# Half-transposes in turns with quarter rows, shared products ahead of the last row, an earlier flag load

## The chip, the cores and the metric

The kernel runs on one core of a Trainium2 chip. The metric is device time in microseconds (us) of one execution. The kernel before took 286.78 us, the median of three runs (286.23 to 288.38).

A core has five engines with a queue each. TensorE (PE in the profile; PEld is its weight load) multiplies matrices into PSUM, VectorE (DVE) and ScalarE (ACT) work element by element and copy out of PSUM, GpSimd (POOL) here mostly issues indirect DMAs, SyncE (SP) issues plain DMAs. An engine takes its instructions in the order of the program and waits on semaphores for the others.

## The reference

One graph convolution with relations and one mixture of experts, on 625 rows of 1024 numbers in float32. Cut to what matters:

```python
# 625 nodes, 20000 edges sorted by dst, 2 edge types
h   = layernorm(x)
n   = ln_weight * h / sqrt(mean(h*h) + 1e-6)
out = n @ W_root + bias                                  # 1024 -> 286
for r in range(2):
    msg  = n[src] @ W_rel[r] * (edge_type == r)
    out += segment_sum(msg, dst) / max(count, 1)
x   = x + h + elu(out) @ wo_weight                       # 286 -> 1024

h2  = layernorm(x)
shared = mean_s( gelu(h2 @ sW1[s] + sb1[s]) @ sW2[s] + sb2[s] )     # 2 shared, 1024 -> 256 -> 1024
gates  = h2 @ rW + rb                                    # 8 experts
w      = softmax of the two largest gates of a row, 0 elsewhere
moe    = sum_e w[:, e] * ( gelu(h2 @ W1[e] + b1[e]) @ W2[e] + b2[e] )
return x + shared + moe
```

## The kernel before

The 625 rows are five row tiles of 125. `sparse_kernel` computes everything under the assumption that edges and expert loads stay within certain sizes; it leaves a flag, and after it `gnn_ffn_kernel` reads the flag into registers and branches to `dense_kernel` where it is above zero (which it isn't with these inputs). The stages of `sparse_kernel`, with the span's time at which the trace shows them:

1. **0 to 94 us, graph convolution.** Edge counts, projection, aggregation.
2. **94 to 122 us, output rows.** The loop over `s` (L1114) does `output_proj(s)` for a row tile; DVE and ACT make the row tile's layer norm h2, two steps later `to_columns` (L835) transposes it on TensorE, eight transposes p_t of 125x125, into `h2T`. h2 is also written to HBM as `h2d`.
3. **122 to 158 us, routing beside the shared experts.** `gate`, `route` and `slots` are a long DVE chain with a few small matmuls: gate logits, the two best experts (`sel`), ranks within an expert (p_rank), the token index of each slot (p_tok), `tok` for whole rows and `tok4` for quarters of rows. TensorE fills its time with `shared_in` (L1202): for each shared expert i, half t and column cut (0..313, 313..625) eight products p_sh (k = 0..7) and a Gelu. The scheduler places these products among the small matmuls; four of the first eight stand ahead of the last row tile's transposes. A register load on TensorE and ACT reads the tiles' expert numbers (`ej`).
4. **158 to 207 us, first expert layer.** Tokens are sorted to 11 tiles of 128 slots: seven whole tiles of one expert (numbers 4 to 10), three of two halves of 64 (0, 1, 2), one of four quarters of 32 (3). They are taken in the order 4, 5, 6, 0, 7, 1, 8, 2, 9, 10, 3. The loop over `s` gives three steps, each a tile behind the one before: `fetch`, `expert_in`, `expert_mid`. `fetch` gathers the tile's rows from `h2d` by POOL's indirect DMA and turns them to columns `xsT`, in one of two ways. A tile in `by_quarters` takes four gathers of 128 x 256 (L1424) and one stream transpose on DVE (L1429). The others take one gather of 128 x 1024 (L1434), eight transposes p_x on TensorE (L1441) into two PSUM banks, a copy of the first four on ACT (L1447) and of the last four on DVE (L1445). Quarter tiles are the places 1, 3, 5, 7, 9, 10 of the order, so the first tile is a whole one. `copy_w1` (L1451) copies second and further experts' w1 for the divided tiles on ACT. `expert_in` (L1458) is the matmuls p_h (16 records for a whole tile) and a DVE copy `hj` (L1466). `expert_mid` (L1471) transposes `hj` on TensorE (p_hT) and applies Gelu on ACT. `xs` has three buffers, `xsT` two; PSUM banks are five for p_x, p_sh and p_yj (`ps_acc`) and three for p_h and p_hT (`ps_mm`).
5. **207 to 245 us, second expert layer.** p_yj (L1522), for each tile two halves of 512 columns; copies `ys` on DVE and ACT (L1526, L1528); a scatter to `yt` in HBM by POOL (L1530).
6. **245 to 288 us, combination.** The shared experts' second layer p_o (L1577, with the biases' row L1579), two halves for each row tile and three parts for the last. SP loads the scattered rows back (g, L1541). `add` (L1549) is a chain on DVE, each held behind the one before: x plus p_o, then x plus weight times g. `store` (L1559) writes a row tile, 112 rows by SP and 13 by ACT. All p_o are held behind the last p_yj (`made`). The flag is loaded to the engines' registers at the end (L1594), then the branch (L1595) and the closing waits (L1624).

What sets the order: `tc.issue_after` holds an instruction behind another one by hand; the rest of each engine's order comes from a scheduler that sees the program as written, and buffers of pools, which add waits on those who used the memory before. `xt`, the pool of `xsT`, is opened after `sh_in` (the shared experts' weights and h2T) is closed.

Of the kernel before, what the change touches and what calls it, by code (L numbers as in the profile page):

```python
# [8 lines left out]
F32 = mybir.dt.float32  # L9
# [9 lines left out]
N = 625  # L19
# [7 lines left out]
TP = 125  # L27
NT = N // TP
KD = D // 128
EP = 125  # L30
EC = E // EP
# [12 lines left out]
NJ = 11  # L44
# [409 lines left out]
def sparse_kernel(  # L454
# [24 lines left out]
    nc = tc.nc  # L479
# [15 lines left out]
    def ps_acc(name):  # L495
        return psum[0].tile([128, 512], F32, tag="acc", name=name, bufs=nacc[0])
# [10 lines left out]
    rows = pool(gnn, "rows", NT)  # L507
# [60 lines left out]
    ident = const.tile([128, 128], F32, name="ident")  # L568
# [311 lines left out]
    made = {}  # L880
# [147 lines left out]
    turned = []  # L1028
# [82 lines left out]

    load_w1(range(2))
    sh_in = ExitStack()
    for s in range(NT + 2):  # L1114
        if s == 0:
            aggregate(NT - 1, 1)
            elu(NT - 1)
            elu_columns(NT - 3)
            cnts.close()
            rt = pool(sh_in, "rt", side="right")  # L1120
            shi = pool(sh_in, "shi", side="right")
            sw1 = shi.tile([128, NS, KD, H], F32, name="sw1")
            for i in range(NS):
                nc.sync.dma_start(sw1[:, i], sW1[i].rearrange("(k p) h -> p k h", p=128))
            load_w1(range(2, NE))
            h2T = shi.tile([128, KD, N], F32, name="h2T")
        if s < NT:
            output_proj(s)
        if s == 0:
            check()  # L1130
        if s < 2:
            elu_columns(NT - 2 + s)
        if 0 <= s - 2 < NT:
            to_columns(s - 2, h2s[s - 2], h2T, False)
    gnn.close()
# [6 lines left out]
    CUTS = ((0, 313), (313, N))  # L1142


    gT = rt.tile([128, 2, TP], F32, name="gT")
    gates = const.tile([TP, NT, NE], F32, name="gates")
# [54 lines left out]

    def shared_in(i, t, then=lambda: None):  # L1202
        b = KD + i * HK + t
        for a, z in CUTS:
            if a:
                then()
            p = ps_acc(f"p_sh_{i}_{t}_{a}")
            for k in range(KD):
                nc.tensor.matmul(p[:, : z - a], sw1[:, i, k, t * 128 : (t + 1) * 128],  # L1209
                                 h2T[:, k, a:z], start=(k == 0), stop=(k == KD - 1))  # L1210
            nc.scalar.activation(shT[:, i, t, a:z], p[:, : z - a], AF.Gelu, bias=vT[:, b : b + 1])


# [164 lines left out]
    def quarter_rows():  # L1378
        own4 = rt.tile([128, 4, 4, QC], F16, tag="above", name="own4")
        tf = rt.tile([128, NJ], F16, name="tf")  # L1380
        for a in range(4):
            nc.scalar.copy(own4[:, a], ident[:, None, a * QC : (a + 1) * QC].to_broadcast([128, 4, QC]))
        with tc.issue_after(named.ins):
            nc.vector.tensor_copy(tf, tok)
        q4 = ps_mm("p_tok4")
        for a in range(4):
            nc.tensor.matmul(q4[:, a * NJ : (a + 1) * NJ], own4[:, a].rearrange("p b r -> p (b r)"), tf,
                             start=True, stop=True)
        nc.vector.tensor_scalar(tok4.rearrange("p a j -> p (a j)"), q4[:, : 4 * NJ], 4.0, quad,
                                op0=ALU.mult, op1=ALU.add)  # L1390

    gate()
    route()
    named = slots()
    weights_T()
    shared_in(1, 0, quarter_rows)
    shared_in(1, 1)
    sh_in.close()

# [15 lines left out]
        return ((0, 128, e_of[NH2 + j - 1]),)  # L1415

    xsT, p_hs, w1m = {}, {}, {}
    acts, turned = [], []

    def fetch(j):  # L1420
        if j in by_quarters:
            xs = io.tile([128, 4, D // 4], F32, tag="io", name=f"xs_{j}")
            for a in range(4):
                nc.gpsimd.indirect_dma_start(  # L1424
                    out=xs[:, a], out_offset=None, in_=h2d.rearrange("n (b f) -> (n b) f", b=4),
                    in_offset=bass.IndirectOffsetOnAxis(ap=tok4[:, a, j : j + 1], axis=0))
            t_ = xt.tile([128, KD, 128], F32, tag="xsT", name=f"xsT_{j}")
            with tc.issue_after(turned[-1].ins):
                nc.vector.transpose(t_.rearrange("p k (a r) -> p a k r", a=4), xs.rearrange("p a (c k) -> p a k c", k=KD))  # L1429
            xsT[j] = t_  # L1430
            copy_w1(j)
            return
        xs = io.tile([128, D], F32, tag="io", name=f"xs_{j}")
        nc.gpsimd.indirect_dma_start(  # L1434
            out=xs, out_offset=None, in_=h2d,
            in_offset=bass.IndirectOffsetOnAxis(ap=tok[:, j : j + 1], axis=0))
        t_ = xt.tile([128, KD, 128], F32, tag="xsT", name=f"xsT_{j}")
        for g in range(2):
            p = ps_acc(f"p_x{g}_{j}")
            for k in range(4):  # L1440
                nc.tensor.transpose(p[:, k * 128 : (k + 1) * 128], xs[:, 4 * g + k :: KD], ident)  # L1441
            o = t_[:, 4 * g : 4 * g + 4, :]
            pv = p.rearrange("p (k n) -> p k n", k=4)
            if g:
                turned.append(nc.vector.tensor_copy(o, pv))  # L1445
            else:
                acts.append(nc.scalar.copy(o, pv))  # L1447
        xsT[j] = t_
        copy_w1(j)

    def copy_w1(j):  # L1451
        for jj, a, e in copies.get(j, ()):
# [28 lines left out]

    whole = range(NM2, NJ)
    tiles = (*whole[:3], 0, whole[3], 1, whole[4], 2, *whole[5:], NH2)
    by_quarters = [tiles[i] for i in (1, 3, 5, 7, 9, 10)]
    copies = {}
    for i, (j, a, e) in zip((1, 3, 5, 6, 8, 9), ((j, a, e) for j in tiles for a, _, e in parts(j)[1:])):
        copies[tiles[i]] = [(j, a, e)]
    for s in range(NJ + 2):
        if s < NJ:
            fetch(tiles[s])  # L1490
        if 0 <= s - 1 < NJ:
            expert_in(tiles[s - 1])
        if 0 <= s - 2 < NJ:
            expert_mid(tiles[s - 2])
# [52 lines left out]
    added = []  # L1547

    def add(*args):  # L1549
        with ExitStack() as order:  # L1550
            if added:
                order.enter_context(tc.issue_after(added[-1].ins))
            added.append(nc.vector.scalar_tensor_tensor(*args, op0=ALU.mult, op1=ALU.add))  # L1553

    def add_experts(d):
# [2 lines left out]

    def store(d, at):  # L1559
        for g, eng in zip(PARTS, (nc.sync, nc.scalar)):  # L1560
            eng.dma_start(out[d * TP + g.start : d * TP + g.stop, at], x1[g, d, at])

    banks = 0
    for d in range(NT):
        if d == LATE:
            for i in range(d, NT):
                add_experts(i)
        own = slice(d * TP, (d + 1) * TP)
        for at in ((0, 512), (512, D)) if d < NT - 1 else ((0, 512), (512, 768), (768, D)):
            n = at[1] - at[0]  # L1570
            at = slice(*at)
            p = (ps_mm if banks % 8 > 4 else ps_acc)(f"p_o_{d}_{at.start}")
            banks += 1
            with tc.issue_after(made.ins):
                for i in range(NS):
                    for k in range(HK):
                        nc.tensor.matmul(p[:TP, :n], shT[:, i, k, own], sw2[:, i, k, at],  # L1577
                                         start=(i == 0 and k == 0), stop=False)
                nc.tensor.matmul(p[:TP, :n], wT[:, own], b23[:, at], start=False, stop=True)  # L1579
            add(x1[:, d, at], p[:TP, :n], 1.0 / NS, x1[:, d, at])  # L1580
            if d == NT - 1:
                store(d, at)
        if d < LATE:
            add_experts(d)
        if d < NT - 1:
            store(d, slice(0, D))


def gnn_ffn_kernel(tc, *args):
    nc = tc.nc  # L1590
    with tc.tile_pool(name="flags", bufs=1) as flags:
        flag = flags.tile([1, 1], I32, name="flag")
        sparse_kernel(tc, flag, *args)
        off = nc.values_load(flag, min_val=0, max_val=EC * 4 + 1)  # L1594
        with tc.If(off > 0):  # L1595
            dense_kernel(tc, *args)

# [30 lines left out]
```

## Time and profile before

| what | value |
|---|---|
| median of three runs | 286.78 us |
| the profiled execution's own time | 290.18 us |
| its span | 288.4 us |
| granted TensorE clock, mean | 0.993 |
| TensorE busy | 277.2 us (96%) |
| DVE busy | 171.8 us (60%) |
| ACT busy | 100.2 us (35%) |
| POOL busy | 65.1 us (23%) |

Busy time is the union of an engine's instructions. The span runs from the first to the last instruction of the profiled execution; the time outside it, 1.8 us here, belongs to the start and end of the launch. A row of a timeline gives start, duration, engine, line, operation, output from input, the number of instructions put together, and in brackets how long the engine was idle before it and who released it. Successive matmuls overlap in the records, so a row's duration is longer than its share of the engine's time.

### The profile page before, as it was taken

To read this page: it belongs to the slowest core of one execution; us is meant where nothing else is said; L and a number is where in the kernel's file an instruction comes from. 1 tells how busy PE (TensorE), PEld (TensorE's weight loads), DVE (VectorE), ACT (ScalarE), POOL (GpSimd) and SP (SyncE) were. 2 spreads that over 40 slices of the span, in tenths; PEclk is the share of its full clock that TensorE was granted. 3 is DMA by queue.
4 is the path that set the end of the run, shared out by engine and by line. 5 is a ranking of instruction groups with operands and counts; after the bars stand their busy time and mean duration, and the time that the engine had idled before them with its cause. 6 is when DMAs were issued, how large, how long until landed. Compare 5 with 4: busy or idle time off the path is not lost.

```text
span 288.4 us, 4459 instructions
## 1 busy us (share of the span) xinstructions
PE 277.2 (96%) x1531; PEld 186.5 (65%) x1531; DVE 171.8 (60%) x433; ACT 100.2 (35%) x232; POOL 65.1 (23%) x128
## 2 busy tenths in 40 slices
PE   8999999999999999899999988999999999999991
PEld 6877777788888455677777877788543344444460
DVE  6899999999874898657800522446143111159820
ACT  3366328243642422453011414854397111000000
POOL 9910110000000124320151656541022222100000
PEclk9999999999999999999999999999999999999997
DMA  7999960000002999996999344321185545399441
GB/s 230 358 333 368 403 216 28 0 0 2 1 0 74 383 391 426 423 403 206 418 406 400 101 145 130 128 60 53 45 338 231 213 190 220 133 374 376 150 142 43
DMA packets 22107, 61.58 MB, mean 214 GB/s; under 512 B 2490, under 2 KB 8317, under 8 KB 21056
## 3 DMA queue, kind: packets, MB, share of 16 engines
q1 hardware_dynamic: 16106, 44.31, 41.3%
q0 software_dynamic: 5680, 16.58, 16.0%
q10 hardware_dynamic: 294, 0.35, 0.6%
q8 instruction: 14, 0.23, 0.3%
q14 instruction: 13, 0.11, 0.1%
HBM read 43.19 MB, written 18.82 MB: 215 GB/s over the span
## 4 chain that ended last, share of the span: by engine, by line
PE 82%; DVE 12%; issue 3%; ACT 1%; DVEq 0%; ACTq 0%
PE p_pr L944 18%; PE p_yj L1522 13%; PE p_o L1577 12%; PE p_h L1462 11%; PE p_sh L1209 11%; PE p_agg L961 5%; PE scrap L1024 2%; PE p_y L1007 2%; DVE xh L1011 2%; PE cnt L923 2%; DVE xsT L1429 1%; DVE st L776 1%; DVE h L749 1%; PE p_t L841 1%; PE p_gate L1155 1%
## 5 line engine op out<-in xcount | busy, mean ns | idle before, releaser
L944 PE MATMUL p_pr<-wg,nT 128*125 128x286 f32 x240 | 61.7, 408 | 0.5 <-ACT nT L847 0.3
L944 PEld LDWEIGHTS p_pr<-wg,nT 128*125 128x125 f32 x240 | 43.4, 187 | 12.7 <-ACT nT L847 1.4
L1462 PE MATMUL p_h<-w1a,xsT 128*128 (+2 forms) x176 | 40.1, 381 | 1.3 <-DVE xsT L1429 1.1
L1522 PE MATMUL p_yj<-w2a,hjT 128*128 (+2 forms) x88 | 38.6, 594 | 0.0
L1577 PE MATMUL p_o<-sw,shT 128*125 128x512 f32 (+1 forms) x88 | 36.1, 553 | 0.0
L1209 PE MATMUL p_sh<-h2T,sw 128*128 128x313 f32 (+1 forms) x128 | 35.3, 429 | 0.0
L1462 PEld LDWEIGHTS p_h<-w1a,xsT 128*128 128x128 f32 (+2 forms) x176 | 28.7, 168 | 8.1 <-issue 1.1
L1209 PEld LDWEIGHTS p_sh<-h2T,sw 128*128 128x128 f32 x128 | 23.6, 189 | 8.5 <-issue 0.2
L1522 PEld LDWEIGHTS p_yj<-w2a,hjT 128*128 128x128 f32 (+2 forms) x88 | 14.4, 168 | 22.4 <-issue 22.4
L1526 DVE COPY ys<-p_yj 128x512 f32<-128x512 f32 x15 | 10.4, 692 | 28.7 <-PE p_yj L1522 26.6
L1577 PEld LDWEIGHTS p_o<-sw,shT 128*125 128x125 f32 x88 | 16.4, 187 | 16.9 <-issue 16.2
L1424 POOL DMA_INDIRECT xs<-h2d,tok x24 | 22.8, 949 | 19.6 <-PE p_x L1441 7.3
L1018 POOL DMA_DIRECT2D x1d<-xh x10 | 5.9, 588 | 71.0 <-DVE flagf L726 62.0
L1466 DVE COPY hj<-p_h 128x256 f32<-128x256 f32 x11 | 4.6, 415 | 27.5 <-PE p_h L1462 12.5
L1530 POOL DMA_INDIRECT yt<-ys,row x11 | 10.7, 973 | 40.8 <-DVE ys L1526 40.8
L1007 PE MATMUL p_y<-wo_t,eT 128*125 128x512 f32 (+1 forms) x40 | 18.8, 592 | 0.0
L1477 ACT ACTIVATE hjT<-p_hT,vT 128x128 f32<-128x128 f32 (+2 forms) x34 | 8.8, 335 | 25.1 <-remote 11.0
L1553 DVE SCALAR_TENSOR_TENSOR x<-p_o,x 125x512 f32<-125x512 f32 (+1 forms) x11 | 6.9, 639 | 15.6 <-PE p_o L1579 15.6
L961 PE MATMUL p_agg<-P,CT 125*125 125x288 f32 x100 | 15.5, 305 | 0.0
L1462 PE MATMUL p_h<-w1m,xsT 128*64 128x256 f32 (+1 forms) x96 | 14.7, 381 | 0.0
L1522 PE MATMUL p_yj<-w2m,hjT 128*64 128x512 f32 (+1 forms) x48 | 14.1, 595 | 0.0
L899 DVE TENSOR_TENSOR ohs<-ohs,cols 125x1024 f16<-125x1024 f16 (+1 forms) x22 | 13.9, 633 | 0.0
(304 smaller groups left out, 412.0 us busy)
## 6 DMA issues: line engine op xcount, KB each, us to landing
w1a<-in_L_ffn_W_dram SPq DMA_DIRECT2D x8, 1024.0 KB
w2a<-in_L_ffn_W_dram SPq DMA_DIRECT2D x8, 1024.0 KB, 5.0
yt<-zero SPq DMA_DIRECT2D x2, 2560.0 KB
g<-yt SPq DMA_DIRECT2D x10, 512.0 KB, 7.3
sw<-in_L_ffn_sW_dram SPq DMA_DIRECT2D x4, 1024.0 KB, 6.2
x<-x1d SPq DMA_DIRECT2D x5, 500.0 KB
x1d<-xh POOLq DMA_DIRECT2D x5, 448.0 KB
h2d<-h POOLq DMA_DIRECT2D x5, 448.0 KB
```

The lines of the kernel that those rows point to most:

```text
L899: last = nc.vector.tensor_tensor(os, os, both(VV_, 128)[1], op=ALU.mult)
L944: nc.tensor.matmul(p[:TP, :F], nT[:, k, m * TP : (m + 1) * TP], wg[:, k, r, :], start=(k == 0), stop=(k == KD - 1))
L961: nc.tensor.matmul(p[:TP, : F + 2], CT[:, m, at : at + TP], P[:, m, r, i], start=(m == 0 and i == 0), stop=(m == NT - 1 and i == 1))
L1007: nc.tensor.matmul(ps[s][:TP, :], eT[:n, k, :], wo_t[:n, k, at], start=(k == 0), stop=False)
L1209: nc.tensor.matmul(p[:, : z - a], sw1[:, i, k, t * 128 : (t + 1) * 128], h2T[:, k, a:z], start=(k == 0), stop=(k == KD - 1))
L1424: nc.gpsimd.indirect_dma_start(out=xs[:, a], out_offset=None, in_=h2d.rearrange("n (b f) -> (n b) f", b=4), in_offset=bass.IndirectOffsetO ...
L1462: nc.tensor.matmul(p[a:b, :H], xsT[j][:, k, a:b], w1m[j, a][:, 0, k, :] if a else w1a[:, bass.ds(e, 1), k, :], start=(k == 0), stop=(k == ...
L1477: done = nc.scalar.activation(hjT[:, j, t, a:b], p[:, t * 128 + a : t * 128 + b], AF.Gelu, bias=bT[:, bass.ds(e, 1), t])
L1522: made = nc.tensor.matmul(p[a:b], hjT[:, j, k, a:b], w2m[j, a, k][:, at] if a else w2a[:, bass.ds(e, 1), k, at], start=(k == 0), stop=(k = ...
L1526: nc.vector.tensor_copy(y[:, at], p)
L1530: sent.append(nc.gpsimd.indirect_dma_start(out=yt, out_offset=bass.IndirectOffsetOnAxis(ap=row[:, j : j + 1], axis=0), in_=y, in_offset=No ...
L1577: nc.tensor.matmul(p[:TP, :n], shT[:, i, k, own], sw2[:, i, k, at], start=(i == 0 and k == 0), stop=False)
```

## The change

Three parts, in the words of the code.

**Shared products.** `shared_products` is the inner loop of `shared_in` with a range of k. In the last step of the output rows' loop, six (`AHEAD`) of the first eight products are called for ahead of the last row tile's `to_columns`; the first call of `shared_in` goes on in the same bank with the other two.

**Turns.** `by_quarters` becomes the places 0, 2, 4, 6, 8, 10 of the same order, that is tiles 4, 6, 7, 8, 9, 3; tiles 5, 0, 1, 2, 10 take TensorE's transposes. `fetch` is split: `gather` issues the DMAs, the first tile's after those of the second; `turn(j, g)` makes four transposes and their copy, the half g = 0 at the tile's own step and g = 1 at the start of the next step, so that the p_h of the tile before stands between the two halves. On TensorE the built program has: p_x0 of 5, p_h of 4, p_x1 of 5, p_h of 5, p_hT of 4, p_x0 of 0, p_h of 6, p_hT of 5, p_x1 of 0, p_h of 0, and so on, and at the end p_h of 10, p_hT of 9, p_h of 3, p_hT of 10, p_hT of 3, then p_yj. The numbers of gathers and transposes of both kinds stay as they were. DVE's first stream transpose is held behind the tok4 computation in place of a p_x copy; the w1 copies move by a place.

**Flag.** The register loads of the flag are called for behind the x1 loads and ahead of the second expert layer, on all engines at once, and the branch uses their value at the end. `add` chains behind DVE's load, `store` behind that of its engine, and p_o of row tiles 2 to 4 behind TensorE's load in place of the last p_yj. In the built program TensorE's load stands after five halves of p_yj; behind it come p_o of row tile 2, columns 512 to 1023, and the first matmul of row tile 3, then the rest of p_yj.

```diff
+    CUTS = ((0, 313), (313, N))
+    AHEAD = 6
+
+    def shared_products(p, i, t, c, ks):
+        a, z = CUTS[c]
+        for k in ks:
+            nc.tensor.matmul(p[:, : z - a], sw1[:, i, k, t * 128 : (t + 1) * 128],
+                             h2T[:, k, a:z], start=(k == 0), stop=(k == KD - 1))
...
+        if s == NT + 1:
+            begun = ps_acc("p_sh")
+            shared_products(begun, 0, 0, 0, range(AHEAD))
         if 0 <= s - 2 < NT:
             to_columns(s - 2, h2s[s - 2], h2T, False)
...
+            first = not (i or t or c)
+            p = begun if first else ps_acc(f"p_sh_{i}_{t}_{a}")
+            shared_products(p, i, t, c, range(AHEAD if first else 0, KD))
...
-    shared_in(1, 0, quarter_rows)
+    turned = []
+    shared_in(1, 0, lambda: turned.append(quarter_rows()))
...
+    def gather(j):
...
+    def fetch(j):
         t_ = xt.tile([128, KD, 128], F32, tag="xsT", name=f"xsT_{j}")
         xsT[j] = t_
+        if j in by_quarters:
+            with tc.issue_after(turned[-1].ins):
+                nc.vector.transpose(t_.rearrange("p k (a r) -> p a k r", a=4), rows[j].rearrange("p a (c k) -> p a k c", k=KD))
+        else:
+            half_row[j] = rows[j]
+            turn(j, 0)
         copy_w1(j)
+
+    def turn(j, g):
+        p = ps_acc(f"p_x{g}_{j}")
+        for k in range(4):
+            nc.tensor.transpose(p[:, k * 128 : (k + 1) * 128], half_row[j][:, 4 * g + k :: KD], ident)
+        o = xsT[j][:, 4 * g : 4 * g + 4, :]
+        pv = p.rearrange("p (k n) -> p k n", k=4)
+        if g:
+            turned.append(nc.vector.tensor_copy(o, pv))
+        else:
+            acts.append(nc.scalar.copy(o, pv))
...
-    by_quarters = [tiles[i] for i in (1, 3, 5, 7, 9, 10)]
+    by_quarters = [tiles[i] for i in (0, 2, 4, 6, 8, 10)]
     copies = {}
-    for i, (j, a, e) in zip((1, 3, 5, 6, 8, 9), ((j, a, e) for j in tiles for a, _, e in parts(j)[1:])):
+    for i, (j, a, e) in zip((2, 4, 6, 7, 8, 9), ((j, a, e) for j in tiles for a, _, e in parts(j)[1:])):
         copies[tiles[i]] = [(j, a, e)]
+    gather(tiles[1])
+    gather(tiles[0])
     for s in range(NJ + 2):
+        if 0 < s <= NJ and tiles[s - 1] in half_row:
+            turn(tiles[s - 1], 1)
         if s < NJ:
+            if s > 1:
+                gather(tiles[s])
             fetch(tiles[s])
...
+    loads, (off,) = nc.values_load_multi_w_load_instructions(flag, min_val=0, max_val=EC * 4 + 1)
+    loads = {load.ins.engine: load for load in loads}
...
-            if added:
-                order.enter_context(tc.issue_after(added[-1].ins))
+            order.enter_context(tc.issue_after((added[-1] if added else loads[mybir.EngineType.DVE]).ins))
...
-            eng.dma_start(out[d * TP + g.start : d * TP + g.stop, at], x1[g, d, at])
+            with tc.issue_after(loads[eng.engine].ins):
+                eng.dma_start(out[d * TP + g.start : d * TP + g.stop, at], x1[g, d, at])
...
-            with tc.issue_after(made.ins):
+            with tc.issue_after((made if d < 2 else loads[mybir.EngineType.PE]).ins):
```

More of the change, by code (lines that the diff above doesn't have):

```diff
@@ L1141, in sparse_kernel @@
         nc.sync.dma_start(w2a[:, e], W2[e].rearrange("(k p) d -> p k d", p=128))
-    CUTS = ((0, 313), (313, N))
     gT = rt.tile([128, 2, TP], F32, name="gT")
@@ L1203, in shared_in @@
         b = KD + i * HK + t
-        for a, z in CUTS:
+        for c, (a, z) in enumerate(CUTS):
             if a:
                 then()
[L1207 to L1210, printed above, removed]
+            first = not (i or t or c)
+            p = begun if first else ps_acc(f"p_sh_{i}_{t}_{a}")
+            shared_products(p, i, t, c, range(AHEAD if first else 0, KD))
             nc.scalar.activation(shT[:, i, t, a:z], p[:, : z - a], AF.Gelu, bias=vT[:, b : b + 1])
@@ L1388, in quarter_rows @@
                              start=True, stop=True)
-        nc.vector.tensor_scalar(tok4.rearrange("p a j -> p (a j)"), q4[:, : 4 * NJ], 4.0, quad,
+        return nc.vector.tensor_scalar(tok4.rearrange("p a j -> p (a j)"), q4[:, : 4 * NJ], 4.0, quad,
                                 op0=ALU.mult, op1=ALU.add)
@@ L1417, in sparse_kernel @@
     xsT, p_hs, w1m = {}, {}, {}
-    acts, turned = [], []
-    def fetch(j):
+    acts = []
+    rows = {}
+    def gather(j):
         if j in by_quarters:
@@ L1426, in fetch @@
                     in_offset=bass.IndirectOffsetOnAxis(ap=tok4[:, a, j : j + 1], axis=0))
[L1427 to L1431, printed above, removed]
+            rows[j] = xs
             return
@@ L1436, in fetch @@
             in_offset=bass.IndirectOffsetOnAxis(ap=tok[:, j : j + 1], axis=0))
+        rows[j] = xs
+    def fetch(j):
         t_ = xt.tile([128, KD, 128], F32, tag="xsT", name=f"xsT_{j}")
[L1438 to L1447, printed above, removed]
-        xsT[j] = t_
-        copy_w1(j)
+        xsT[j] = t_
+        if j in by_quarters:
[4 more added lines that the diff above has]
+            turn(j, 0)
+        copy_w1(j)
+    half_row = {}
+    def turn(j, g):
[8 more added lines that the diff above has]
+            acts.append(nc.scalar.copy(o, pv))
     def copy_w1(j):
@@ L1586, in sparse_kernel @@
             store(d, slice(0, D))
+    return off
 def gnn_ffn_kernel(tc, *args):
@@ L1592, in gnn_ffn_kernel @@
         flag = flags.tile([1, 1], I32, name="flag")
-        sparse_kernel(tc, flag, *args)
-        off = nc.values_load(flag, min_val=0, max_val=EC * 4 + 1)
+        off = sparse_kernel(tc, flag, *args)
         with tc.If(off > 0):
```

## The prediction

> **What bounds the kernel now.** I read the page first: the engines' shares and the chain that ended last.
>
> ```profile
> PE 277.2 (96%) x1531; PEld 186.5 (65%) x1531; DVE 171.8 (60%) x433; ACT 100.2 (35%) x232; POOL 65.1 (23%) x128
> ...
> PEclk9999999999999999999999999999999999999997
> ...
> PE 82%; DVE 12%; issue 3%; ACT 1%; DVEq 0%; ACTq 0%
> ```
>
> TensorE works for 96% of the span at full granted clock, and the chain is on it for 82%. The change neither adds nor removes a matmul, a transpose or a gather, so all it can do is close or open gaps of TensorE, and move what follows TensorE's last instruction. I therefore went through the PE timeline stage by stage for those gaps. Rows give start, duration, then the idle time in brackets. Ends of matmuls are modelled and overlap, so a gap is counted from start to start: the distance to the next start, less the steady pace of that kind.
>
> The front, where the last rows of h2 are turned:
>
> ```profile
> 117.63 2.28 PE L1209 MATMUL p_sh<-h2T,sw 128*128 128x313 f32 x8
> 120.80 1.04 PE L841 MATMUL p_t<-ident,h 125*128 125x125 f32 x8 [0.90 <-DVE h L749]
> ```
>
> Eight records are four shared products (two records each) at 0.265 us a record. A ninth record would have started at 119.75; the transposes start at 120.80, when DVE has row tile 4 of h. The gap is 1.05 us.
>
> The expert stage, TensorE, then DVE and POOL beside it:
>
> ```profile
> 158.09 1.06 PE L1441 MATMUL p_x<-ident,xs 128*128 128x128 f32 x8
> 159.37 3.72 PE L1462 MATMUL p_h<-w1a,xsT 128*128 x16 [0.23 <-ACT xsT L1447]
> ...
> 171.96 0.44 PE L1474 MATMUL p_hT<-ident,hj 128*128 128x128 f32 x2 [0.85 <-issue]
> 172.24 1.05 PE L1441 MATMUL p_x<-ident,xs 128*128 128x128 f32 x8
> 174.04 0.40 PE L1462 MATMUL p_h<-w1a,xsT 128*64 x1 [0.75 <-DVE xsT L1429]
> ```
>
> ```profile
> 159.79 2.04 DVE L1429 STREAM_TRANSPOSE xsT<-xs 128x1024 f32<-128x1024 f32 x1
> ...
> 171.82 2.07 DVE L1429 STREAM_TRANSPOSE xsT<-xs 128x1024 f32<-128x1024 f32 x1
> ```
>
> ```profile
> 159.41 0.95 POOL L1424 DMA_INDIRECT xs<-h2d,tok  x1 [7.25 <-PE p_x L1441]
> 160.66 0.94 POOL L1424 DMA_INDIRECT xs<-h2d,tok  x1 [0.30 <-issue]
> ```
>
> From 158.09 to 206.51 (the end of the last p_h) the excess over pace, start to start, is 0.40 and 0.10 at the first tile, 1.02 at 171.96, 0.92 at 174.04, then 0.11, 0.49 (at 191.50, a DVE transpose again), 0.08 and 0.09: **3.21 us**. After 206.51 TensorE has no gap until its last matmul at 281.7. That is followed by the last add, a store and closing waits to 288.4.
>
> The tail on DVE:
>
> ```profile
> 260.80 10.16 DVE L1553 SCALAR_TENSOR_TENSOR x<-g,wab,x 125x1024 f32<-125x1024 f32 x8
> 270.87 1.88 DVE L1553 SCALAR_TENSOR_TENSOR x<-p_o,x 125x512 f32<-125x512 f32 x3
> 274.68 0.69 DVE L1553 SCALAR_TENSOR_TENSOR x<-p_o,x 125x512 f32<-125x512 f32 x1 [1.94 <-PE p_o L1579]
> 278.34 0.69 DVE L1553 SCALAR_TENSOR_TENSOR x<-p_o,x 125x512 f32<-125x512 f32 x1 [2.96 <-PE p_o L1579]
> ...
> 282.02 0.42 DVE L1553 SCALAR_TENSOR_TENSOR x<-p_o,x 125x256 f32<-125x256 f32 x1 [1.42 <-PE p_o L1579]
> ```
>
> DVE waits for TensorE at 274.68, 278.34 and 282.02: there is slack before each, and the last add is released by TensorE.
>
> **Part 1, six shared products ahead of the last row.** The built program now has six products before the eight transposes where it had four, and eight afterwards, before the ranks, where there were ten. Four more records at 0.265 us are 1.06 us: 119.75 + 1.06 = 120.81, against 120.80 at which the transposes start now. So the gap closes, the transposes and the gate behind them are late by 0.01 us, and 1.05 us of products is gone from later. It counts only if nothing later waits for something unmoved. TensorE reaches the rank matmuls at 131.13; sel, their input, is ready at 128.91, so 130.09 is still after it. The DVE chain to the token indices starts from these ranks (131.86) and ends at 140.13, 0.05 us before TensorE's token matmuls at 140.18; both ends move together. The gathers start from it too and move along. Gain **1.04 us**. Bounds: 0 (if the transposes' copies were met by a bank not yet free) and 1.05.
>
> **Part 2, the turns.** New order on TensorE: half of the transposes of whole tile 5, p_h of tile 4, the other half, p_h of tile 5, and so on; DVE makes tiles 4, 6, 7, 8, 9, 3 by its transpose.
>
> *Start.* The tile pool of xsT opens where the shared products' weights and h2T lay, and in the built program DVE's transpose of tile 4 waits for the last shared product. So it starts at 158.30 (0.05 after the products' end at 158.25, on the clock of before) and takes 2.06; at 160.36 + 0.14 (the step seen at 173.90 to 174.04) p_h_4 starts, at 160.50. Only four transposes, 0.44 us, are left to cover this: they end at 158.53. Cost **1.97 us**, in place of the 0.50 at this point before. The four gathers of tile 4 are issued until 149.96; whole gathers issued at 142.34 and 151.21 beside the w2 traffic landed 7.2 and 7.4 us later, so the last of tile 4 lands about 157.3, before 158.30. If it is 1 us later than that, it costs nothing; beyond, what it is late.
>
> *Middle.* Every DVE transpose now runs beside a p_h of 3.62 us and needs 2.06 plus a hidden-layer copy of 0.42 and a half copy of 0.69: 3.17, within it. The waits at 171.96 (own hidden copy), 174.04 and 191.50 should go: 2.43 us. A quarter tile's four gathers take 5.0 us of POOL (1.25 apart) plus about 2.45 to land, and start when the second half of a whole tile's transposes has freed its room; against the new order this leaves 2.4 us or more, and 0.6 to 1.2 us at the transposes themselves. ACT's copies of w1 (2.17 each) stay covered by two tiles' time. I keep 0.30 for small waits as seen (0.08 to 0.11 each at three places); bounds 0 and, if each of five turns waits as at 191.50, 5 x 0.49 = 2.45.
>
> The Trainium skill, "SBUF — State Buffer", section "SBUF: two separate sides", speaks against more pairs of DVE transposes and gathers in turns: a DVE operation in a two-port mode locks GpSimd out of writing descriptors, and the section below it gives some 620 ns becoming some 3100 ns. By it each of six transposes could add an estimated 2.5 us to one gather, which alone would use up the slack above and leave about no gain. The row above decides against it: the issue at 160.66 ran inside the transpose of 159.79 to 161.83 and took 0.94 us, as the one before it.
>
> *End.* Before, two p_yj records stood between the last hidden transposes of tiles 10 and 3; now these two follow p_h_3 back to back, so p_hT_3 waits for DVE's copy of p_h_3: the 0.42 us copy, and 0.16 to its start, against 0.22 of the other transposes. Cost **0.42 us** (bounds 0 and 0.6).
>
> Sum of the stage: 1.97 + 0.30 + 0.42 = 2.69 against 3.21, gain **0.52 us**. With all bounds: from 2.39 (gain 0.8) to 1.97 + 2.45 + 0.6 = 5.0 (loss 1.8).
>
> **Part 3, flag and shared output.** The register loads of the flag leave the tail. On TensorE one stands after five p_yj halves; behind it p_o of row tile 2's second half and one matmul of row tile 3 are pulled forward: 3.66 + 0.86 = 4.52 us of the same work, done earlier. They need sw2: asked for at 206.63 and 207.05, landed by 211.2 and 214.0, needed at 206.5 + 9.5 = 216.0 or later. No wait. The load itself took 0.32 us (flag) and 1.57 us (expert numbers, 155.22) on TensorE's queue, which runs some 3.5 us ahead of the array (278.16 beside matmuls until 281.97): 0; uncovered 0.32 to 1.57. On SP, ACT and DVE what is queued behind the loads (sw2, stores, adds) comes long after. In the tail the loads were beside the last store, on which SP waits until 286.36: removing them is worth 0.
>
> What pays is the order: p_yj's rest, its scatters, the loads of g and the adds move 4.52 us back. The eight g adds end at 275.5 in place of 270.96; four more adds (0.6 apart) end at about 277.9. TensorE ends row 4's first half at 278.3 as before, so DVE is on time with 0.4 us to spare there and 3.0 us at the last add. Stores of rows 2 and 3 now leave at 276.7 and 277.9, in place of 272.18 and 275.40, 448 KB each, landing 3.3 us later; the last store (112 KB) leaves at 282.47. I take 0.1 us; bounds 0 and 1.5 (a last store that lands as late as these large ones).
>
> **Sum.** 1.04 + 0.52 - 0.1 = 1.46 us off the profiled execution: 290.18 (span 288.4 and 1.8 around it) to 288.72. The median shown is 286.78, 1.2% under that execution; scaled by 286.78 / 290.18, 288.72 becomes **285.3 us**.
>
> **Rivals.**
> 1. *The turns cover all.* Small waits and the end wait vanish: stage excess 1.97, gain 1.04 + 1.24 = 2.3, so 284.5; with the transpose of tile 4 also hidden, 4.2, so 282.6. For it: 3.17 us fit within 3.62. Against: the wait on the last shared product stands in the program. Chance 0.14, a third of it for the second.
> 2. *The turns only move the waits.* The start costs 1.97 and the turns wait 1.5 to 2.0 in sum for gathers or copies: stage 4.0 to 4.4, loss about 1.0 us, which eats part 1: 286.8. For it: slack of 0.6 us at each transpose is thin. Against: measured copies fit. Chance 0.20.
> 3. *Slower: the tail becomes DVE's.* All g adds come 4.5 us later; if g's ten loads land a further 3.0 us late (they took 7.3 us as a median), the last add is DVE's, and every microsecond beyond is paid. To be slower than before needs 3.0 + 1.5 = 4.5 us; 7 us late would give 290.18 - 1.5 + 4.0 = 292.7, so 289.3. Against: the same loads behind the same scatters. Chance 0.09.
>
> The forecast has 0.57. A measurement of this kernel tells about 1% from no change, here 283.9 and 289.7. Faster: rival 1's second form, 0.05, and 0.02 of its first. Slower: half of rival 3, 0.04, and 0.02 for the far end of the stage's bounds. Range 283.9 to 287.7: below it lies 0.07, above it 0.11 (rival 3 and 0.02 of rival 2).
>
> **What would show it.** Right: no idle time ahead of the last eight p_t at L841; the first p_h at about 159.5 waiting for DVE's transpose by about 1.9 us; no idle time over 0.3 us at L1462 afterwards; p_hT of the last tile waiting for hj; p_o rows inside the p_yj stretch; DVE nearly without idle time before row 4's first add. Wrong: a first p_h released by DMA, quarter gathers (L1436 of the changed kernel) late at several turns, TensorE idle inside p_yj at the early p_o, or a last add released by DVE or DMA.

## The result

The changed kernel takes 288.63 us (median of 22 runs, 287.89 to 289.59) where the kernel before took 287.59 us beside it (22 runs, 286.02 to 288.79). The ratio is **1.0042, 95% interval 1.0028 to 1.0056**: 1.2 us slower, where 1.5 us faster was forecast. Medians and ratios here are of fast runs of both kernels from one chip, those within 1.5% of the fastest of their kernel; on the second chip of the experiments such runs still hold copies that start late (last section), so its ratios (r5 to r8, r13 to r16) say less than the stage lengths. The profiled execution of the changed kernel took 288.16 us, span 286.4.

The page of the changed kernel: engines, and the chain that ended last.

```profile
PE 276.6 (97%) x1531; PEld 185.3 (65%) x1531; DVE 172.0 (60%) x433; ACT 100.4 (35%) x232; POOL 64.7 (23%) x128
...
PE 90%; DMA 3%; DVE 3%; SPq 1%; issue 0%; ACT 0%
```

The chain went from 82% to 90% TensorE. By these two profiles alone the change looks like a gain of 2 us. That contradiction with the timed runs is what the experiments had to settle. First what the change did, row by row. TensorE at the front (start, duration; a bracket would show idle time):

```profile
117.29 3.33 PE L1120 MATMUL p_sh<-h2T,sw 128*128 128x313 f32 x12
120.47 1.04 PE L841 MATMUL p_t<-ident,h 125*128 125x125 f32 x8
```

Twelve records, and the transposes follow without idle time: the gap of 1.05 us is closed. TensorE at the start of the expert stage:

```profile
156.69 0.61 PE L1463 MATMUL p_x<-ident,xs 128*128 128x128 f32 x4
158.98 3.72 PE L1482 MATMUL p_h<-w1a,xsT 128*128 x16 [1.68 <-DVE xsT L1452]
162.54 0.60 PE L1463 MATMUL p_x<-ident,xs 128*128 128x128 f32 x4
162.97 3.62 PE L1482 MATMUL p_h<-w1a,xsT 128*128 x16
```

The first p_h waits for DVE's transpose of tile 4: 158.98 - 156.69 is 2.29 us from start to start, and less 0.44 for the four transposes it is 1.85 us of waiting. After it the stage runs without waits worth naming, up to its end:

```profile
204.16 0.44 PE L1494 MATMUL p_hT<-ident,hj 128*128 128x128 f32 x2
204.90 0.41 PE L1494 MATMUL p_hT<-ident,hj 128*128 128x128 f32 x2 [0.30 <-DVE hj L1486]
205.49 8.82 PE L1550 MATMUL p_yj<-w2a,hjT 128*128 x20 [0.18 <-issue]
```

0.74 and 0.59 us between starts, against a pace of 0.22: 0.89 us lost. DVE at the tail:

```profile
263.87 10.16 DVE L1580 SCALAR_TENSOR_TENSOR x<-g,wab,x 125x1024 f32<-125x1024 f32 x8
273.94 2.48 DVE L1580 SCALAR_TENSOR_TENSOR x<-p_o,x 125x512 f32<-125x512 f32 x4
276.89 0.69 DVE L1580 SCALAR_TENSOR_TENSOR x<-p_o,x 125x512 f32<-125x512 f32 x1 [0.48 <-PE p_o L1607]
...
280.57 0.42 DVE L1580 SCALAR_TENSOR_TENSOR x<-p_o,x 125x256 f32<-125x256 f32 x1 [1.42 <-PE p_o L1607]
```

DVE still waits for TensorE before row 4's three adds, 0.48 us at the first: the last add is TensorE's.

### The profile page after: what moved, and what is told of

It reads as the page before. It is cut to its first block, busy times and chain, and to the rows that moved or that the text cites. A ratio compares the mean times of both kernels' runs of the same rounds, so it can differ in the third digit from the quotient of the medians.

```text
span 286.4 us, 4456 instructions
## 1 busy us (share of the span) xinstructions
PE 276.6 (97%) x1531; PEld 185.3 (65%) x1531; DVE 172.0 (60%) x433; ACT 100.4 (35%) x232; POOL 64.7 (23%) x128
## 4 chain that ended last, share of the span: by engine, by line
PE 90%; DMA 3%; DVE 3%; SPq 1%; issue 0%; ACT 0%
PE p_pr L944 18%; PE p_h L1482 14%; PE p_yj L1550 13%; PE p_o L1605 12%; PE p_sh L1120 12%; PE p_y L1007 6%; PE p_agg L961 5%; DMA xh<-in_x_dram 3%; PE p_t L841 2%; PE cnt L923 2%; PE p_x L1463 1%; DVE st L776 1%; PE p_hT L1494 1%; PE p_gate L1165 1%; PE p_y L1008 1%; PE p_o L1607 1%
## 5 line engine op out<-in xcount | busy, mean ns | idle before, releaser
L1452 DVE STREAM_TRANSPOSE xsT<-xs 128x1024 f32<-128x1024 f32 x6 | 12.3, 2051 | 12.4 <-PE p_sh L1120 12.4
```

## The experiments

Runs r1 to r4 shared one chip, r5 to r8 a second, r9 to r12 a third, and r13 to r16 the second again. The stage lengths are differences of TensorE's rows: A from the first p_sh to the first p_x, B from there to the first p_yj, C from there to the end of the last p_o. S is their sum, in us. Where p_yj has an early first half, only S is given. Which chip the first profile and the main comparison came from isn't known; the unchanged kernel's median in that comparison, 287.59 us, is near those of the first and third chip (287.66 and 287.10).

| run | what | A | B | C | S | ratio to before, 95% |
|---|---|---|---|---|---|---|
| profile shown of before | | 40.46 | 48.69 | 75.20 | 164.35 | |
| r1 | before once more | 40.46 | 46.36 | 75.20 | 162.02 | 0.9997, 0.9973 to 1.0020 |
| changed kernel | | 39.40 | 48.80 | 75.05 | 163.25 | 1.0042, 1.0028 to 1.0056 |
| r2 | shared products alone | 39.41 | 46.35 | 75.20 | 160.96 | 0.9956, 0.9933 to 0.9978 |
| r3 | turns alone | 40.47 | 47.73 | 75.20 | 163.40 | 1.0056, 1.0031 to 1.0082 |
| r4 | flag part alone | 40.46 | 47.41 | 75.05 | 162.92 | 1.0026, 1.0008 to 1.0044 |
| r5 | turns, own room | 40.45 | 46.10 | 75.20 | 161.75 | 0.9954, 0.9926 to 0.9983 |
| r6 | flag part, filler back | | | | 163.38 | 1.0031, 0.9993 to 1.0069 |
| r7 | all three, both mended | | | | 160.92 | 0.9931, 0.9896 to 0.9965 |
| r8 | shared products, turns with own room | 39.41 | 46.18 | 75.20 | 160.79 | 0.9922, 0.9892 to 0.9952 |
| r9 | changed kernel, own room | 39.41 | 46.81 | 75.05 | 161.27 | 0.9994, 0.9959 to 1.0029 |
| r10 | changed kernel, filler back | | | | 162.36 | 1.0060, 1.0036 to 1.0083 |
| r11 | r8 again | 39.41 | 45.80 | 75.20 | 160.41 | 0.9944, 0.9912 to 0.9976 |
| r12 | r2 again | 39.41 | 46.35 | 75.20 | 160.96 | 0.9971, 0.9945 to 0.9998 |
| r13 | flag loads alone | | | | 166.75 | 1.0033, 0.9996 to 1.0070 |
| r14 | flag loads, filler back | | | | 164.43 | 1.0000, 0.9967 to 1.0033 |
| r15 | r6 again | | | | 166.53 | 1.0054, 1.0018 to 1.0090 |
| r16 | changed kernel again | 39.41 | 48.88 | 75.05 | 163.34 | 0.9910, 0.9881 to 0.9939 |

**The kernel before once more, and each part alone.** r1 is the file of before, unchanged. r2, r3 and r4 each apply one part of the change to it, without the other two. The diffs are cut to what matters, with `...` where lines are left out:

For r2:

```diff
...
+        if s == NT + 1:
+            begun = ps_acc("p_sh")
+            shared_products(begun, 0, 0, 0, range(AHEAD))
...
```

For r3, with `gather`, `fetch` and `turn` as in the change:

```diff
-    by_quarters = [tiles[i] for i in (1, 3, 5, 7, 9, 10)]
+    by_quarters = [tiles[i] for i in (0, 2, 4, 6, 8, 10)]
...
+        if 0 < s <= NJ and tiles[s - 1] in half_row:
+            turn(tiles[s - 1], 1)
...
```

For r4, with `add` and `store` behind the loads as in the change:

```diff
+    loads, (off,) = nc.values_load_multi_w_load_instructions(flag, min_val=0, max_val=EC * 4 + 1)
...
-            with tc.issue_after(made.ins):
+            with tc.issue_after((made if d < 2 else loads[mybir.EngineType.PE]).ins):
...
```

> The unchanged kernel against itself: a ratio within 0.3% of 1. The profile shown of before took 290.18 us, more than any of its 22 timed runs (median 287.59), so a second profile should show where some 2.5 us of that one execution lay. Theory A (that execution was late in one place that the change also touches): its expert stage or its tail is shorter here. Theory B (late everywhere or in the front): the stages from 117 us on are as in the first profile and the front or the time outside the span differs.

> Only the six shared products ahead of the last row's transposes. Theory A (TensorE's gaps add up, as in the prediction): 1.0 us less, ratio 0.9965. Theory B (the token chain or gathers do not move along, or something later gives it back): 1.00. Theory C (this part is what makes the whole slower): ratio 1.003 or more.

> Only the turns of quarter tiles and half-transposes. Theory A: by the sums of the prediction 0.5 us less (0.998); by the profile of the changed kernel, whose expert stage was 48.80 us against 48.69, no change (1.000). Theory C (this part makes the whole slower, since in most runs of before the expert stage is shorter than in the profile shown): 1.004 to 1.007.

> Only the earlier flag loads, with one and a quarter p_o in the midst of p_yj. Theory A: between 0.5 us less (by the tails of the two profiles, 5.85 against 6.42 us behind the last matmul) and 0.1 us more: 0.998 to 1.0005. Theory C (this part makes the whole slower through the later scatters, loads of g and bunched stores): 1.004 to 1.007, with the last add or the last store later than 6.4 us behind the last matmul.

r1 settles the contradiction. Its stages A and C are those of the first profile to 0.01 us, but B is 46.36 us in place of 48.69. The first p_x of the first profile starts at 158.09; its first p_yj, and both rows in r1:

```profile
206.78 1.02 PE L1522 MATMUL p_yj<-w2a,hjT 128*128 x2
```

```profile
157.49 1.06 PE L1441 MATMUL p_x<-ident,xs 128*128 128x128 f32 x8
...
203.85 1.02 PE L1522 MATMUL p_yj<-w2a,hjT 128*128 x2
```

The 2.33 us lay in the expert stage of the one execution that the prediction was built on. DVE's timeline in that first profile, copies of the hidden layer:

```profile
163.12 0.42 DVE L1466 COPY hj<-p_h 128x256 f32<-128x256 f32 x1 [1.30 <-PE p_h L1462]
...
171.48 0.42 DVE L1466 COPY hj<-p_h 128x256 f32<-128x256 f32 x1 [6.72 <-PE p_h L1462]
...
173.81 0.39 DVE L1466 COPY hj<-p_h 128x256 f32<-128x256 f32 x1
...
179.85 0.42 DVE L1466 COPY hj<-p_h 128x256 f32<-128x256 f32 x1 [5.06 <-remote]
```

and in r1, the same program:

```profile
162.53 0.42 DVE L1466 COPY hj<-p_h 128x256 f32<-128x256 f32 x1 [1.29 <-PE p_h L1462]
...
166.89 0.42 DVE L1466 COPY hj<-p_h 128x256 f32<-128x256 f32 x1 [2.71 <-PE p_h L1462]
...
170.56 0.42 DVE L1466 COPY hj<-p_h 128x256 f32<-128x256 f32 x1 [1.29 <-PE p_h L1462]
...
175.29 0.42 DVE L1466 COPY hj<-p_h 128x256 f32<-128x256 f32 x1 [2.87 <-PE p_h L1462]
```

In r1 every copy starts 0.04 to 0.10 us after the end of its p_h. In the first profile the second copy starts at 171.48 although its p_h ended at 167.44; TensorE's next hidden transposes and DVE's next stream transpose, in order behind it, are the waits of 171.96 and 174.04 that the prediction gave to the order of the tiles. The wait at 191.50 is of the same kind: the copy ahead of that stream transpose starts at 188.94, 2.7 us after its p_h. Theory A of r1 holds: late in one place, which the change also touches.

The three parts add up. By S, against r1: -1.06 (r2), +1.38 (r3), +0.90 (r4), together +1.22; the changed kernel's S is 1.23 more than r1's, and 0.42% of 287.59 is 1.2 us. By ratios, -1.3, +1.6 and +0.7 us. The shared products do what was forecast; both other parts cost. r3 is as its theory C says. r4's ratio, 1.0026, lies between its theories, and its span ends 5.3 us behind the last matmul, not later than 6.4: what the flag part costs here stands in TensorE's rows, 1.05 us more in B and 0.15 less in C.

**What the turns cost.** Is it the wait at the start? The transposed columns of tile 4 are laid where the shared weights sw1 were, which the last shared product still reads. One tile for each shared expert, expert 0's in the place that the columns will take, removes that wait, since expert 0's last product is long done:

```diff
...
-            sw1 = shi.tile([128, NS, KD, H], F32, name="sw1")
+            sw1 = {i: shi.tile([128, KD, H], F32, name=f"sw1_{i}") for i in (1, 0)}
             for i in range(NS):
-                nc.sync.dma_start(sw1[:, i], sW1[i].rearrange("(k p) h -> p k h", p=128))
+                nc.sync.dma_start(sw1[i], sW1[i].rearrange("(k p) h -> p k h", p=128))
...
```

> The turns alone, with the first shared weights cut into one tile for each shared expert, so that the room that tile 4's columns take was last read by shared expert 0 and DVE's first transpose no longer waits for the last shared product. Theory P (that wait is what the turns cost): from the first p_x to the first p_yj 45.9 us, against 47.7 for the turns alone and 46.4 for the kernel before; ratio 0.998 to 0.999. Theory Q (the turns cost elsewhere, gathers or copies between tiles): still 47.0 us or more, ratio 1.004 or more.

DVE and then TensorE in r3 (turns alone):

```profile
159.20 2.03 DVE L1443 STREAM_TRANSPOSE xsT<-xs 128x1024 f32<-128x1024 f32 x1 [12.39 <-PE p_sh L1209]
```

```profile
159.00 0.61 PE L1454 MATMUL p_x<-ident,xs 128*128 128x128 f32 x4
161.28 3.72 PE L1473 MATMUL p_h<-w1a,xsT 128*128 x16 [1.68 <-DVE xsT L1443]
```

and in r5 (own room):

```profile
155.66 2.04 DVE L1443 STREAM_TRANSPOSE xsT<-xs 128x1024 f32<-128x1024 f32 x1 [9.98 <-DMA xs<-h2d,tok]
```

```profile
157.86 0.61 PE L1454 MATMUL p_x<-ident,xs 128*128 128x128 f32 x4
158.30 3.62 PE L1473 MATMUL p_h<-w1a,xsT 128*128 x16
```

The transpose is now released by its gathers, at 155.66, 2.2 us before TensorE's first p_x, and p_h follows the four transposes without a gap. B falls from 47.73 to 46.10, where theory P had 45.9: the wait for the shared products was what the turns cost. With the room, the turns are worth 0.2 to 0.6 us of B against 46.36 (r5, r8 and r11). The ratio of 0.9954 is below what theory P said. S is only 0.27 us under r1's, which would be 0.999; on this chip the unchanged kernel takes longer (last section).

**What the flag part costs.** In the program of r4 the last two hidden transposes stand next to each other, as in the changed kernel; before, a p_yj product stood between them. r6 calls for a p_yj half ahead of the last `expert_mid`, and leaves it out of the later loop:

```diff
...
+        if s == NJ + 1:
+            p_first = ps_acc("p_yj_first")
+            for k in range(HK):
+                for a, b, e in parts(tiles[0]):
+                    nc.tensor.matmul(p_first[a:b], hjT[:, tiles[0], k, a:b], w2a[:, bass.ds(e, 1), k, 0:512],
+                                     start=(k == 0), stop=(k == HK - 1))
         if 0 <= s - 2 < NJ:
             expert_mid(tiles[s - 2])
...
```

> The flag part alone, with tile 4's first half of the second layer called for ahead of the last tile's hidden transposes, so that it stands between the last two of these again. Theory P (this lost filler is what the flag part costs): from the last p_h's end to the first p_yj 0.2 us, against 1.26 in the flag part alone; ratio 0.999 to 1.000. Theory Q (the cost lies in the late scatters, loads of g and stores): ratio 1.002 or more.

> The changed kernel with both of these edits. If both theories P hold, TensorE's sum is 1.05 (front) + 0.45 (turns) + 0.15 (flag) less than before: ratio 0.994, 285.9 us. If they don't, it stays at or above that of the shared products alone (0.9956).

> The shared products ahead and the turns with their own room, without the flag part. Theory P: 1.5 us less than before, ratio 0.995, within 0.2 us of all parts mended, since the flag loads are off the path at both places. If the later scatters and stores of the flag part cost something by themselves, this one is the faster by that.

In r6 the filler is back on TensorE: 0.21 us from the last p_h's end to the first p_yj, as theory P says, against 1.25 in r4. Its time left the rest open: 1.0031, with an interval over both answers, and its profile is one with late copies as above, so its S can't be compared. r7 and r8 beat both kernels; r7's S is 1.1 us under r1's, where 1.65 was forecast, and r8's 1.2, where 1.5 was. r8, without the flag part, has the lower median (285.86 in seven runs against 286.64), but the two intervals overlap. So no gain of the mended flag part is shown.

**The two losses apart, on a third chip.** r9 and r10 mend one of the two in the changed kernel; r11 and r12 repeat r8 and r2.

> The changed kernel with the own room for tile 4's columns alone. If the two losses are apart and add up: TensorE's sum is 1.05 and 0.2 less and 0.9 more than before, 0.3 to 0.4 us less, ratio 0.9985, some 1.6 us under the changed kernel. If the room is not the cause: ratio 1.004, as the changed kernel.

> The changed kernel with the filler between the last hidden transposes alone. If the losses add up: 1.05 less and 1.35 more than before, 0.3 us more, ratio 1.001, some 0.9 us under the changed kernel. If the flag part costs by its late stores: ratio 1.003 or more.

> The shared products ahead and the turns with their own room, once more and beside the shared products alone on the same chip. If the mended turns are worth what TensorE's rows say, 0.2 us under the shared products alone, ratio 0.9945 to 0.996; if the whole gain against before is the front's, no difference to them.

> The shared products alone, as before: 1.05 us less, ratio 0.996. On a chip whose unchanged kernel shows late releases of DVE and ACT in the expert stage, as the profile of before does, it should show them too (its order there is the unchanged one), and the turns of the run beside it should not pay for them.

In r9 S is 2.0 us under the changed kernel's, so the room is the cause there too; it is 0.75 us below r1's, where the forecast had 0.3 to 0.4, and the interval of its ratio, 0.9959 to 1.0029, holds both. r11 against r12: S 0.55 us less, medians 285.58 and 286.26; by these rows the mended turns are worth about half a microsecond on top of the shared products, though the two intervals overlap. r12's expectation of late copies was not put to the test, for this chip showed none. r10 was a miss in time: S is 0.34 us more than r1's, as forecast, but by ratio it takes 1.0 to 2.4 us more. Its filler is in place, and its span ends 6.4 us behind the last matmul, where r11 and r12 have 5.1 and 5.3: something behind the matmuls costs.

**Loads and pulled p_o apart.** r13 leaves every p_o behind the last p_yj and keeps the early loads; r14 adds the filler; r15 is r6 once more, r16 the changed kernel. r13 against r4:

```diff
-            with tc.issue_after((made if d < 2 else loads[mybir.EngineType.PE]).ins):
+            with tc.issue_after(made.ins):
```

> Of the flag part the early loads alone: every p_o stays behind the last p_yj. The filler between the last two hidden transposes is lost here too. If the filler is the cause: TensorE 1.05 us more from p_h to p_yj, stores as in the kernel before, ratio 1.003 to 1.004. If the pulled p_o is the cause: 1.000.

> The same with the filler put back. The loads alone should then cost nothing: ratio 0.999 to 1.001. If it stays at 1.003, a load of a register early on some engine costs by itself.

> The flag part with the filler put back and p_o of row tile 2's second half pulled forward. TensorE's sum is that of before. If the bunched stores cost what the landings of three profiles suggest, 0.8 us: ratio 1.002 to 1.004, with 3.7 us or more from the last store's issue to its landing; if not, 1.000 and about 3.0 us.

> The changed kernel once more: 1.003 to 1.006. By the ledger: 1.05 less (front), 1.4 more (turns), 1.05 more (filler), 0.15 less (one step between p_yj and p_o), and 0.1 to 0.3 more for the stores, in sum 1.4 us.

The early loads alone lose the filler (TensorE in r13), and r14 has it back:

```profile
208.72 0.44 PE L1474 MATMUL p_hT<-ident,hj 128*128 128x128 f32 x2
209.45 0.41 PE L1474 MATMUL p_hT<-ident,hj 128*128 128x128 f32 x2 [0.29 <-DVE hj L1466]
210.00 1.52 PE L1524 MATMUL p_yj<-w2a,hjT 128*128 x3
```

```profile
206.08 0.44 PE L1474 MATMUL p_hT<-ident,hj 128*128 128x128 f32 x2
206.35 1.88 PE L1497 MATMUL p_yj_first<-w2a,hjT 128*128 x4
208.07 0.38 PE L1474 MATMUL p_hT<-ident,hj 128*128 128x128 f32 x2
208.29 1.88 PE L1530 MATMUL p_yj<-w2a,hjT 128*128 x4
```

In r13 the filler is gone although TensorE's own load stands at its old place near the end (281.2 us; 277.7 in r14), where no p_o waits for it: calling for the loads earlier was enough. r14 is at 1.0000, interval 0.9967 to 1.0033, and behind its last p_h the profile is r1's (0.20 us to the first p_yj, 75.20 from there to the end of the last p_o): no cost of the earlier loads on ACT and DVE is shown. r15, with p_o pulled forward as well, is at 1.0054; the two intervals overlap. DVE at the tail of r15 shows what differs:

```profile
269.03 10.15 DVE L1560 SCALAR_TENSOR_TENSOR x<-g,wab,x 125x1024 f32<-125x1024 f32 x8
279.10 3.08 DVE L1560 SCALAR_TENSOR_TENSOR x<-p_o,x 125x512 f32<-125x512 f32 x5
283.04 0.42 DVE L1560 SCALAR_TENSOR_TENSOR x<-p_o,x 125x256 f32<-125x256 f32 x1 [0.86 <-PE p_o L1587]
```

The eight g adds end so late that five p_o adds queue up behind them, row 4's first among them, and rows 2, 3 and the first of row 4 are stored 4.4, 3.2 and 2.6 us before the last matmul's end, against 9.8, 6.6 and 2.9 in r1. From the last store's issue to the clearing of SP's wait for it took 3.7 to 4.0 us in the four profiles with filler and pulled p_o (r6, r7, r10, r15), 2.8 to 3.4 in the four with pulled p_o and no filler (the changed kernel, r4, r9, r16), and 2.5 to 3.9 (mean 3.1) in the ten without pulled p_o. So pulling p_o forward gains nothing on TensorE (r13, without it, has C at 75.05 as r4 has) and, with the filler in place, the last store takes 0.8 us longer by the means of few profiles; that the stores close before it are the reason is argued, not shown. For r10, 0.34 and 0.8 make 1.1, inside its interval of 1.0 to 2.4 us. Against r12 on the same chip its profile has 1.4 us more in S and 1.1 behind the last matmul, in sum 2.5, as the medians (288.78 and 286.26).

r16 is the surprise: on this chip the changed kernel is the **faster** one, 288.33 against 290.17, ratio 0.991 (0.9881 to 0.9939), where 1.003 to 1.006 was forecast. Its own stages are those of the first measurement (B 48.88 against 48.80); it is the unchanged order that takes longer here (last section).

## Why the prediction was wrong, point by point

**The step that failed is "the excess over pace ... 3.21 us" of the expert stage, and with it "the waits at 171.96 ..., 174.04 and 191.50 should go: 2.43 us".** The excess is what that one execution shows, and the program has it neither in r1 nor in r2, r4 and r12, which keep its order of the tiles: 48.69 - 3.21 is 45.48 us of pace, so r1's 46.36 has 0.88 us of excess. Of the 2.43 us that the turns were to save in the middle, 2.33 was not there to be saved. The profiled execution stood at 290.18, above the slowest of the runs shown (288.38), and the text divided this out by a factor. The difference was not a scale on all stages; it sat in the very waits that the change was credited with. That the unscaled forecast, 288.72, lies 0.1 from the measured median is luck: TensorE's sum came out 0.46 us above what it had (163.25 against 164.35 less 1.04 and 0.52), and the span ended 5.85 us behind the last matmul, not 6.42.

The way from 1.46 us faster to 1.2 slower is then, by TensorE's sum: 2.33 us that were not there to save, 0.48 more at the end of the stage, 0.11 more at small waits, 0.12 less at the start, and the 0.1 forecast for the stores, which S doesn't have. All signs of "Right" came true in the changed kernel's profile, but none of them looked at the kernel before.

**Part 1 was right.** 1.04 us was forecast; A is 1.05 shorter, and the gate, ranks and gathers moved along. The transposes show no wait.

**The start of the turns was right**: 1.97 forecast, 1.85 measured. So were the small waits of the middle: r3's B is 47.73 - 45.48 = 2.25 us over pace, 1.84 for the start and 0.41 for the rest, against 0.30. The last gather of tile 4 was there earlier than the 157.3 forecast: in r5, with its own room, the transpose that waits for it starts at 155.66. After the first tile no DVE transpose of the changed kernel's profile held TensorE up for a gather.

The rule of the Trainium skill ("SBUF — State Buffer", "SBUF: two separate sides") on DVE locking out GpSimd's descriptor writing is for operations in a two-port mode. No such delay showed with these stream transposes, as the row of the prediction had said: in the changed kernel four gathers' issues lie wholly inside a transpose and took 0.94 to 0.95 us each, the one at 172.89, for example, inside that of 172.07 to 174.14.

**The end of the stage was mis-sized and put down to the wrong part.** 0.42 us was forecast, with the turns. r3 does not have it, r4 and r13 do: with the flag's loads called for ahead of p_yj, the scheduler puts the last hidden transposes side by side. It costs 0.90 in S, not 0.42: the second transpose is 0.52 late, for the copy, and the first p_yj another 0.37 behind it, where only the copy had been counted. Why the p_yj is late isn't shown.

**Flag and p_o**: no wait at the early p_o, right (p_o starts at 214.15 as the fifth half of p_yj ends). DVE on time with 0.4 us to spare: 0.48 measured. The loads' removal from the tail worth 0: r14 agrees, within its 0.33% for the loads that moved. The bunched stores were counted at 0.1 in the changed kernel; the spread of the landings is too wide to tell 0.1 from 0.4 there.

**Rivals.** Rival 2, waits moved into the turns, did not come: it had 4.0 to 4.4 us of excess in the stage, where 48.80 - 45.48 = 3.3 is measured, and 1.5 to 2.0 of waits at the turns, where r3 has 0.41. Rival 3, a tail that becomes DVE's, did not come. What no rival said was that the baseline's waits belonged to the execution.

## What to carry to other kernels

When the profiled execution is slower than the timed runs beside it, find out in which rows before crediting a change with removing them: a wait that another execution of the same program does not have can't be gained. A change of order in one place (here register loads called for earlier) can shift what a scheduler uses as filler between two dependent instructions elsewhere; compare the built order around every dependent pair, not only where the edit is. And a first producer that inherits its room from the last consumer of the stage before waits for it; here cutting one tile in two and laying the earlier-free half underneath took 1.6 us away, and with it and without the flag part the kernel is at 0.994 of before on the third chip (r11) and 0.992 on the second (r8), where the kernel before has late copies.

## What the runs showed of the hardware that was not expected

On the second chip, and in the first profile, DVE and ACT were released late by TensorE in the expert stage of the unchanged order: copies started up to 4.8 us after their p_h (r13; 4.0 in the first profile), while on two other chips every profile has 0.04 to 0.10 us. The trace names the releaser "remote" in some of these, and between 160 and 195 us the first profile holds 15 to 30 records of semaphore updates in each 5 us (numbers 100 and up), and r13 to r16 hold 12 to 36, where r1 holds 53 to 69. DVE and ACT are released within 0.05 us of each other (172.86 and 172.91 in r15, 4.7 and 4.6 us after the p_h and p_hT that they wait for), which speaks for the signal and against one engine's queue; it is argued, not shown. From the first p_x to the end of the last p_h the unchanged order took 47.5 to 50.7 us there (r6, r13, r14, r15), against 46.15 in r1.

The turned order has late copies on that chip too. DVE in r16, tiles 1 and 2:

```profile
185.89 0.43 DVE L1486 COPY hj<-p_h 128x256 f32<-128x256 f32 x1 [3.21 <-remote]
187.82 0.42 DVE L1486 COPY hj<-p_h 128x256 f32<-128x256 f32 x1 [1.51 <-PE p_h L1482]
...
194.42 0.42 DVE L1486 COPY hj<-p_h 128x256 f32<-128x256 f32 x1 [3.21 <-remote]
```

They are 2.4 and 2.3 us behind their p_h (0.95 at tile 0), but B is 48.88 against 48.80 without them: behind a late copy DVE's queue holds another copy there, where the unchanged order has a stream transpose that the next p_h needs. r5, r7 and r8 have copies up to 3.8 us late, and from the first p_x to the end of the last p_h they take 45.9 to 46.1 us, against 45.6 in r9 and r11 on the third chip. So the turns do cover most of the waits that were forecast to go, but only where there are such waits. What makes the signals late was not tried and stays open.
